# Graph attention on one core: a bound on the gathered index, empty places' logits set by VectorE, and another order of the tiles

## Chip, cores, metric

The kernel runs on one core of one Trainium2 chip. The metric is the device time of one execution in microseconds; the kernel before takes 5479.6 us, the median of three runs (5479.25 to 5485.96).

## What is computed

The input is a graph of 10000 nodes and 170000 edges, sorted by the node that they end in (`dst`); every node has an edge to itself among them. Two graph-attention layers follow each other, with a residual and a normalisation each:

```python
def gat_conv(x, edge_index, W, a_src, a_dst, bias, heads, out_ch, concat):
    xl = (x @ W).reshape(n, heads, out_ch)
    alpha_src = einsum('nhc,hc->nh', xl, a_src)
    alpha_dst = einsum('nhc,hc->nh', xl, a_dst)
    e = leaky_relu(alpha_src[src] + alpha_dst[dst], 0.2)
    e = exp(e - segment_max(e, dst)[dst])
    alpha = e / (segment_sum(e, dst)[dst] + 1e-16)
    return segment_sum(xl[src] * alpha, dst) + bias

h = relu(layer_norm(gat_conv(x, 768 -> 4 heads of 256))) + x @ Wr1 + br1
h = layer_norm(gat_conv(h, 1024 -> 1 head of 768)) + h @ Wr2 + br2
out = layernorm(x + h)
```

All numbers are 32-bit floats. For each node the rows `xl[src]` of its neighbours (17 on average) must be fetched, weighed by the softmax of their logits and added up.

## The kernel before

**Tables and places.** A row of a table holds a node's projected features and its logits: 1024 + 4 + 4 floats in `table1`, 768 + 1 + 1 in `table2`, the source logits first and then the destination logits. One float more in `table1` is the node's rank. Nodes are ranked by falling degree (`prepare`, beside the first projection), and 128 ranks make a tile, 79 in all. A tile t has a fixed number of places n = `SLOTS[t]` for each of its nodes (`slot_counts`, L61): 41 in tile 0, 27 in tile 1, down to 8 in tile 78, 1377 in all. Place 0 is the node itself, the others its neighbours. A node with fewer neighbours than its tile has places points at row `NP` in the places left over. Row `NP` of both tables (`none`, L606 to L611) has features 0 and logits of -1e30, so that its weight becomes 0; its rank field holds `NP`.

**Order.** `TURNS` (L96) is the order in which both layers walk the tiles: 78, 76, ... 0, then 1, 3, ... 77, so the sizes grow from 8 to 41 and fall again to 9. `FIRST[t]` is a tile's first place in that order.

**Ring.** A `Ring` (L434) holds the rows of 28 places in layer 1 and 38 in layer 2 for 128 nodes at once. `fetch` issues one indirect DMA of GpSimd (POOL) for a place: 128 rows, one a partition, named by the column `slots[:, q]` (the gather of L418). A place's gather is issued as soon as the place 28 (or 38) before it has been used up. In layer 2 a tile's own rows lie in a row in `table2`, and SP loads them (L445).

**A tile.** `logits` (L461) adds the source logits of the gathered rows and the tile's own destination logits on VectorE (DVE), for one or two stretches of the ring (`ring.parts`), takes leaky relu and the maximum, and has ScalarE (ACT) take the exponential. In layer 1 ACT also copies the rank field of the gathered rows into `slots` (L478): this is the list of rows that layer 2 gathers, since `table2` is ordered by rank. `normalised` divides the weights by their sum. Then the rows are weighed and added: in layer 1 the first few places of a tile on TensorE through diagonal matrices (L703, L709), of the others one in four by DVE alone (L508) and three by ACT and DVE (L497, L504); in layer 2 512 columns on DVE (L508) and 256 on TensorE (L859, L860). The next tile's logits are taken while this tile is being weighed, if it fits in the ring (L795, L924). Tile 0 doesn't fit and goes through `attend_parts` in three parts.

**Around it.** In layer 1 each tile's sum is normalised (L550 to L566), joined with the residual product (L765), transposed and multiplied by W2 (L169), and stored to `table2` (L730). Layer 2 starts when `table2` is complete. In layer 2 a tile's residual product (L871, L874) uses `h1_d` and a gathered x; DVE adds it on L884, and an indirect DMA of POOL with a bound scatters the result to `out` (L893).

The order of instructions on every engine is that of the program (`manual_schedule`).

Of the kernel before, what the change touches and what calls it, by code (L numbers as in the profile page):

```python
# [78 lines left out]
def gnn_kernel(ctx, tc, x, x_cols, src, dst, src_col, dst_col, W1, a_src1, a_dst1, b1, g1, be1, Wr1, br1,  # L79
               W2, a_src2, a_dst2, b2, g2, be2, Wr2, br2, out, n_edges):  # L80
    nc = tc.nc
    N, D0 = out.shape
    H1, DH1 = a_src1.shape
# [9 lines left out]
    CAPS = slot_counts(N, n_edges)  # L93
    SLOTS = CAPS

    TURNS = list(range(NT - 1, -1, -2))  # L96
    TURNS += sorted(set(range(NT)) - set(TURNS))
    FIRST, TOTAL = [0] * NT, 0
    for t in TURNS:
# [88 lines left out]
    def prepare():  # L188

        with tc.tile_pool(name="prep", bufs=1, side="right") as pool, \  # L190
# [107 lines left out]
                base, s = more, 2 * s  # L298
            nc.vector.tensor_sub(base, base, each)
            rank = pool.tile([P, NT], F32, name="rank")  # L300
            to = pool.tile([P, NT], I32, name="to")
            written = 0

# [33 lines left out]
            with nc.allow_non_contiguous_dma(reason="16 bytes a node"):  # L337
                for to, d in zip([sorted_] + others, order_d):
                    nc.sync.dma_start(to, d.rearrange("(t p) f -> p t f", p=P))
                    yield  # L340
                nc.sync.dma_start(table1[:NP, R1 - 1:].rearrange("(p j) r -> p (j r)", p=P), rank)
                yield
            for other in others:
                nc.vector.tensor_add(sorted_, sorted_, other)
# [89 lines left out]
    class Ring:  # L434

        def __init__(self, pool, table, row, size, own):
            self.table, self.size, self.own, self.issued = table, size, own, 0
            self.rows = pool.tile([P, size, row], F32, name="ring")  # L440

        def fetch(self, upto):
            for q in range(self.issued, min(upto, TOTAL)):
                if q in self.own:
                    nc.sync.dma_start(self.slot(q), self.table[self.own[q] * P:(self.own[q] + 1) * P, :])  # L445
                else:
                    gather(self.slot(q), self.table[:, :], slots[:, q:q + 1])
                self.issued = q + 1

        def slot(self, q):  # L450
# [10 lines left out]
    def logits(small, ring, lo, hi, ad, heads, c, top=None):  # L461


        n = hi - lo
        e = small.tile([P, ring.size, heads], F32, name="e")[:, :n]
        for a, b, rows in ring.parts(lo, hi):
            nc.vector.tensor_tensor(e[:, a - lo:b - lo], rows[:, :, c:c + heads],
                                    ad[:, None, :].to_broadcast([P, b - a, heads]), op=OP.add)
        leaky(e, e)
        new = small.tile([P, heads], F32, name="new")  # L470
        nc.vector.reduce_max(new, e.rearrange("p k h -> p h k"), axis=AX.X)
        if top is not None:
            nc.vector.tensor_max(new, new, top)
        nc.vector.tensor_tensor(e, e, new[:, None, :].to_broadcast([P, n, heads]), op=OP.subtract)  # L474
        nc.scalar.activation(e, e, AF.Exp)  # L475
        if not ring.own:
            for a, b, rows in ring.parts(lo, hi):
                nc.scalar.copy(slots[:, a:b], rows[:, :, R1 - 1])  # L478
        return e, new

    def normalised(small, e, heads, t):
# [109 lines left out]
    with tc.tile_pool(name="w1", bufs=1) as w1p, tc.tile_pool(name="l1", bufs=2) as io, \  # L591
            psum_for_products(), tc.manual_schedule():
        w1 = w1p.tile([P, K0, C1], F32, name="w1")
        xTs = {}

        def load_x(t):
            if t < NT:
                xTs[t] = io.tile([P, K0, P], F32, name="xT", bufs=3)
                nc.sync.dma_start(xTs[t], x_cols[t])

        load_x(0)
        for k in range(K0):
            nc.sync.dma_start(w1[:, k, :], W1[k * P:(k + 1) * P, :])
        load_x(1)
        as_b, ad_b = spread(w1p, a_src1, "as1_b"), spread(w1p, a_dst1, "ad1_b")
        none = w1p.tile([P, R1], F32, name="none")[:1]  # L606
        nc.vector.memset(none[:, :C1], 0.0)
        nc.vector.memset(none[:, C1:], -BIG)
        nc.vector.memset(none[:, R1 - 1:], float(NP))
        nc.scalar.dma_start(table1[NP:NP + 1, :], none)  # L610
        nc.scalar.dma_start(table2[NP:NP + 1, :], none[:, C1 - C2:C1 + 2 * H2])  # L611


        b1_b = w1p.tile([P, R1], F32, name="none")[:, :C1]
        nc.scalar.dma_start(b1_b, bass.AP(tensor=b1.tensor, offset=b1.offset, ap=[[0, P], [1, C1]]))

        def weight_steps():

            with nc.allow_non_contiguous_dma(reason="1024 numbers"):
                nc.scalar.dma_start(br1_c, br1.rearrange("(k p) -> p k", p=P))
            yield
            yield
            brT = spread_br1(w1p, "brT")
            load(w2, W2)
            for i, a in enumerate((a_src2, a_dst2)):
                vec = spread(w1p, a, "a2")
                for k in range(K1):
                    yield  # L630
                    m = io.tile([P, C1], F32, name="scr")[:, :C2]
                    nc.vector.tensor_mul(m, w2[:, k, :C2], vec)
                    nc.scalar.activation(m, m, AF.Copy, accum_out=w2[:, k, C2 + i:C2 + i + 1])
            load(wr1, Wr1)
            yield
            q = product(brT, w2, R2)
            row = io.tile([P, R1], F32, name="row")
            nc.scalar.copy(row[:, :R2], q[:, :R2])
            nc.vector.tensor_add(lift, row[:, C2:C2 + 1], row[:, C2 + 1:R2])
            nc.scalar.dma_start(shift, row[0:1, :C2])  # L640


        steps = itertools.zip_longest(prepare(), weight_steps())
        for t in range(NT):
            p = product(xTs.pop(t), w1, C1)
            row = io.tile([P, R1], F32, name="row")
            nc.scalar.copy(row[:, :C1], p[:, :C1])  # L647
            for i, vec in enumerate((as_b, ad_b)):
# [19 lines left out]
    def ordered_layer1():  # L668
        nonlocal ps_big
        with tc.tile_pool(name="b1", bufs=1) as pool, tc.tile_pool(name="small1", bufs=2) as small, \  # L670
# [20 lines left out]
            def weights_of(t):  # L691

                n, m = SLOTS[t], on_pe(t)
                e, _ = logits(small, ring, FIRST[t], FIRST[t] + n, ring.slot(FIRST[t])[:, C1 + H1:C1 + 2 * H1], H1, C1)
                yield e
                normalised(small, e, H1, t)

# [34 lines left out]
            for t in range(NT + 1):  # L732
# [54 lines left out]
                if live and not whole:  # L787
                    due(n)
                    acc = ps_acc.tile([P, 2 * BANK], F32, name="acc")
                    ad = small.tile([P, H1], F32, name="ad")  # L790
                    nc.vector.tensor_copy(ad, ring.slot(FIRST[t])[:, C1 + H1:C1 + 2 * H1])
# [22 lines left out]
    def ordered_layer2():  # L814
        nonlocal ps_big
        with tc.tile_pool(name="b2", bufs=1) as pool, tc.tile_pool(name="small2", bufs=2) as small, \
# [28 lines left out]
            def weights_of(t):  # L845
# [1 line left out]

                n = SLOTS[t]
                ad = small.tile([P, H2], F32, name="ad")
                nc.vector.tensor_add(ad, ring.slot(FIRST[t])[:, C2 + H2:], lift)  # L850
# [53 lines left out]
            for t in range(NT):  # L904
# [4 lines left out]
                if not whole(t):  # L909
                    for _ in last:  # L910
                        pass
                    ad = small.tile([P, H2], F32, name="ad")
                    nc.vector.tensor_add(ad, ring.slot(FIRST[t])[:, C2 + H2:], lift)
# [34 lines left out]
    def general_path():  # L948
# [82 lines left out]
        def attend_chunks(keep, work, small, lists, table, row, heads, dh, t):  # L1031
# [7 lines left out]
            nc.vector.tensor_copy(top, acc[:, c:c + heads])  # L1039
# [3 lines left out]
            nc.vector.tensor_copy(adm[:, :heads], acc[:, c + heads:c + 2 * heads])  # L1043
# [7 lines left out]
            with tc.For_i(lo, hi, G) as i:  # L1051
# [19 lines left out]
                for g in range(0, G, zg):  # L1071
                    z = work.tile([P, zg, heads, P], F32, name="z")
                    nc.vector.tensor_tensor(
                        z, off[:, g:g + zg, None, :].to_broadcast([P, zg, heads, P]),
                        xg[:, g:g + zg, c:c + heads, None].to_broadcast([P, zg, heads, P]), op=OP.add)
# [22 lines left out]
                nc.vector.tensor_add(e, xg[:, :, c:c + heads], sel[:, :, :heads])  # L1098
# [118 lines left out]
```

## Time and profile before

| | |
|---|---|
| median of three runs | 5479.6 us |
| the profiled execution | 5488.77 us, span 5487.0 us, mean granted clock 0.938 |
| busy share of the span | PE 87%, DVE 79%, POOL 59%, ACT 57% |
| first projection and ranking | 0 to some 905 us |
| layer 1 | some 905 to 3490 us |
| layer 2 | some 3490 to 5487 us |
| DMA packets | 457866, 1581.74 MB, mean 288 GB/s |
| gathers into the ring (L418) | 2675, mean 969 ns of POOL |

The profile is one execution. "Busy" counts the time in which an engine executes; the sequencer's work between two instructions is not in it, and shows as idle time before the next. A wait is put down to the instruction whose signal came last.

### The profile page before, as it was taken

What the parts mean: (1) busy time and instruction counts of PE and PEld (TensorE: products, weight loads), DVE (VectorE), ACT (ScalarE), POOL (GpSimd) and SP (SyncE); (2) the same over time, 40 slices, a digit from 0 to 9 for tenths busy, and PEclk for the clock granted to TensorE, in tenths of its full rate; (3) what the DMA queues carried; (4) which work ended last, traced back from release to release, by engine and by line L of the source; (5) the groups of instructions that cost most, each with busy time, mean ns of one, the idle gap of its engine ahead of it and who ended that gap; (6) DMA issues with size and microseconds to landing.
All of it is one profiled execution on the core that took longest, in us unless ns stands there. A gap on an engine that the chain in (4) does not pass through costs nothing. (4 is left out here: it accounts for less than half of the span.)

```text
span 5487.0 us, 58297 instructions
## 1 busy us (share of the span) xinstructions
PE 4754.0 (87%) x15032; PEld 2827.1 (52%) x15032; DVE 4328.8 (79%) x7766; ACT 3148.0 (57%) x8255; POOL 3247.4 (59%) x3238
## 2 busy tenths in 40 slices
PE   8999997999999875478999999799988746888998
PEld 3444443555555543245555555466655524555665
DVE  5784244899998888788999999498877786778998
ACT  3433344788888877678888888244433312333444
POOL 2445455455566555455665554377777775777774
PEclk9999998999999988789999999899998877899999
DMA  4333625899999988789999997699999987999996
GB/s 152 124 95 82 94 91 202 316 328 339 339 361 347 344 303 301 285 315 345 353 359 347 341 329 263 239 340 360 345 333 321 336 297 258 331 323 349 349 355 240
DMA packets 457866, 1581.74 MB, mean 288 GB/s; under 512 B 111851, under 2 KB 116011, under 8 KB 457526
## 3 DMA queue, kind: packets, MB, share of 16 engines
q0 software_dynamic: 328704, 1339.21, 68.3%
q1 hardware_dynamic: 126768, 235.29, 13.1%
q10 hardware_dynamic: 2054, 3.42, 0.2%
q8 instruction: 126, 2.06, 0.2%
q14 instruction: 214, 1.75, 0.1%
HBM read 1431.80 MB, written 146.23 MB: 288 GB/s over the span
## 5 line engine op out<-in xcount | busy, mean ns | idle before, releaser
L418 POOL DMA_INDIRECT ring<-table,slots x2675 | 2591.7, 969 | 1635.6 <-DVE acc L508 402.4
L508 DVE SCALAR_TENSOR_TENSOR acc<-ring,e,acc 128x256 f32<-128x256 f32 (+1 forms) x2538 | 1572.0, 619 | 127.5 <-PE acc L709 52.0
L497 ACT ACTIVATE ring<-ring,e 128x256 f32<-128x256 f32 x3320 | 1351.0, 505 | 0.0
L504 DVE TENSOR_TENSOR acc<-acc,ring 128x1024 f32<-128x1024 f32 x830 | 1022.5, 1232 | 72.8 <-ACT ring L497 1.2
L874 PE MATMUL big<-wr,w 128*128 128x512 f32 (+1 forms) x2528 | 857.9, 493 | 0.0
L169 PE MATMUL big<-w,xT 128*128 128x512 f32 x1896 | 827.7, 598 | 28.9 <-DMA w<-in_W_dram 11.2
L169 PE MATMUL big<-wr,xT 128*128 128x512 f32 x1896 | 834.1, 596 | 0.7 <-ACT xT L575 0.7
L169 PE MATMUL big<-w,hT 128*128 128x512 f32 (+1 forms) x2528 | 832.1, 486 | 1.2 <-ACT hT L575 1.2
L860 PE MATMUL big<-ring,diagonals 128*128 128x256 f32 x2672 | 660.8, 409 | 185.3 <-ACT diagonals L859 177.0
L860 PEld LDWEIGHTS big<-ring,diagonals 128*128 128x128 f32 x2672 | 543.6, 206 | 299.4 <-ACT diagonals L859 201.2
L169 PEld LDWEIGHTS big<-w,hT 128*128 128x128 f32 x2528 | 478.4, 189 | 375.0 <-issue 341.3
L709 PE MATMUL acc<-ring,diagonals 128*128 128x256 f32 x1816 | 456.6, 409 | 247.9 <-ACT diagonals L703 216.5
L874 PEld LDWEIGHTS big<-wr,w 128*128 128x128 f32 x2528 | 488.1, 193 | 350.3 <-issue 317.7
L169 PEld LDWEIGHTS big<-w,xT 128*128 128x128 f32 x1896 | 362.7, 192 | 491.9 <-issue 472.8
L169 PEld LDWEIGHTS big<-wr,xT 128*128 128x128 f32 x1896 | 356.9, 192 | 421.2 <-issue 420.3
L709 PEld LDWEIGHTS acc<-ring,diagonals 128*128 128x128 f32 x1816 | 370.1, 206 | 326.8 <-ACT diagonals L703 235.7
L859 ACT ACTIVATE diagonals<-ident,e 128x128 f32<-128x128 f32 x1336 | 399.6, 387 | 155.6 <-DVE e L488 117.9
L554 ACT ACTIVATE sd<-mv,eps 128x1 f32<-128x1 f32 x237 | 69.8, 294 | 614.0 <-DVE mv L552 613.6
L650 DVE TENSOR_TENSOR scr<-big,as_b 128x1024 f32<-128x1024 f32 x79 | 96.8, 1225 | 391.9 <-ACT row L647 391.9
L655 POOL TENSOR_TENSOR row<-row,none 128x1024 f32<-128x1024 f32 x79 | 187.2, 2369 | 280.5 <-ACT row L647 279.9
L703 ACT ACTIVATE diagonals<-ident,e 128x128 f32<-128x128 f32 x908 | 278.5, 387 | 96.4 <-DVE e L488 96.4
L475 ACT ACT_TABLE_LOAD x153 | 196.3, 1283 | 233.1 <-DVE e L474 205.9
(172 smaller groups left out, 3895.5 us busy)
## 6 DMA issues: line engine op xcount, KB each, us to landing
ring<-table,slots POOLq DMA_INDIRECT x2675, 6.5
table<-row SPq DMA_DIRECT2D x79, 516.0 KB, 3.6
h_d<-hT SPq DMA_DIRECT2D x79, 512.0 KB, 7.2
w<-h_d SPq DMA_DIRECT2D x79, 512.0 KB, 8.4
table<-row SPq DMA_DIRECT2D x79, 385.0 KB, 6.2
ring<-table SPq DMA_DIRECT2D x79, 385.0 KB, 6.5
xT<-in_x_cols_dram SPq DMA_DIRECT2D x79, 384.0 KB, 4.5
wr<-in_Wr_dram SPq DMA_DIRECT2D x2, 3072.0 KB
```

The costliest lines, as they stand in the source:

```text
L169: nc.tensor.matmul(p[:, c:e], aT[:, j, :], w[:, j, c:e], start=(j == 0), stop=(j == k - 1))
L418: nc.gpsimd.indirect_dma_start(out=to, out_offset=None, in_=table, in_offset=bass.IndirectOffsetOnAxis(ap=index, axis=0), **more)
L475: nc.scalar.activation(e, e, AF.Exp)
L497: nc.scalar.activation(row[:, s], row[:, s], AF.Copy, scale=e[:, h:h + 1])
L504: nc.vector.tensor_add(acc[:, :c], acc[:, :c], row[:, :c])
L508: nc.vector.scalar_tensor_tensor(acc[:, s], row[:, s], e[:, h:h + 1], (acc if first is None else first)[:, s], op0=OP.mult, op1=OP.add)
L655: nc.gpsimd.tensor_add(row[:, :C1], row[:, :C1], b1_b)
L703: nc.scalar.activation(diagonals[:, k * H1 + i, :], ident, AF.Copy, scale=e[:, k, i:i + 1])
L709: nc.tensor.matmul(acc[:, c:d], diagonals[:, k * H1 + i, :], ring.slot(FIRST[t] + k)[:, c:d], start=(k == 0 and c % BANK == 0), stop=(k == ...
L859: nc.scalar.activation(diagonals[:, k % G, :], ident, AF.Copy, scale=e[:, k, :])
L860: nc.tensor.matmul(to, diagonals[:, k % G, :], ring.slot(FIRST[t] + k)[:, ON_PE2:C2], start=False, stop=(k == n - 1), skip_group_check=True)
L874: nc.tensor.matmul(r[:, c:d], hT[:, j, :], wr2[:, j, c:d], start=False, stop=(j == K1 - 1 and (d < C2 or not whole(t))), skip_group_check= ...
```

## The change

Three parts. First, the gathers into the ring get a bound, `NP - 1`: a row whose index is `NP` is not fetched, and the place keeps what it held. The first 28 (or 38) places, which fill the ring, are gathered without the bound. Second, since a place that is not fetched must still have a logit of -1e30, DVE sets the logit columns of the ring to -1e30 once they have been used; for this the destination logits come first in a row now and the source logits second, next to the rank. The rank is stored as a negative number, so that the same -1e30 becomes `NP` by a multiplication with -1 and a minimum with `NP`, which DVE does in place of ACT's copy. Third, `TURNS` becomes 78, 77, ... 48, then 47, 45, ... 1, then 0, 2, ... 46: sizes 8 to 16 in steps of one tile, up to 41, and down to 16.

```diff
-    TURNS = list(range(NT - 1, -1, -2))
+    TURNS = list(range(NT - 1, NT * 3 // 5, -1)) + list(range(NT * 3 // 5, -1, -2))
     TURNS += sorted(set(range(NT)) - set(TURNS))
...
-                nc.sync.dma_start(table1[:NP, R1 - 1:].rearrange("(p j) r -> p (j r)", p=P), rank)
+                nc.vector.tensor_scalar(less_rank, rank, -1.0, None, op0=OP.mult)
+                nc.sync.dma_start(table1[:NP, R1 - 1:].rearrange("(p j) r -> p (j r)", p=P), less_rank)
...
                 if q in self.own:
                     nc.sync.dma_start(self.slot(q), self.table[self.own[q] * P:(self.own[q] + 1) * P, :])
+                elif q < self.size:
+                    gather(self.slot(q), self.table[:, :], slots[:, q:q + 1])
                 else:
-                    gather(self.slot(q), self.table[:, :], slots[:, q:q + 1])
+                    gather(self.slot(q), self.table[:, :], slots[:, q:q + 1], bounds_check=NP - 1,
+                           oob_is_err=False)
...
-            nc.vector.tensor_tensor(e[:, a - lo:b - lo], rows[:, :, c:c + heads],
+            nc.vector.tensor_tensor(e[:, a - lo:b - lo], rows[:, :, c + heads:c + 2 * heads],
                                     ad[:, None, :].to_broadcast([P, b - a, heads]), op=OP.add)
...
         nc.scalar.activation(e, e, AF.Exp)
-        if not ring.own:
-            for a, b, rows in ring.parts(lo, hi):
-                nc.scalar.copy(slots[:, a:b], rows[:, :, R1 - 1])
+        for a, b, rows in ring.parts(lo, hi):
+            if not ring.own:
+                nc.vector.tensor_scalar(slots[:, a:b], rows[:, :, R1 - 1], -1.0, float(NP), op0=OP.mult, op1=OP.min)
+            nc.vector.memset(rows[:, :, c + heads:], -BIG)
...
-        nc.vector.memset(none[:, R1 - 1:], float(NP))
```

The other lines of the diff only swap the two groups of logit columns where they are written and read.

More of the change, by code (lines that the diff above doesn't have):

```diff
@@ L300, in prepare @@
             rank = pool.tile([P, NT], F32, name="rank")
+            less_rank = pool.tile([P, NT], F32, name="less_rank")
             to = pool.tile([P, NT], I32, name="to")
@@ L626, in weight_steps @@
             load(w2, W2)
-            for i, a in enumerate((a_src2, a_dst2)):
+            for i, a in enumerate((a_dst2, a_src2)):
                 vec = spread(w1p, a, "a2")
@@ L647, in gnn_kernel @@
             nc.scalar.copy(row[:, :C1], p[:, :C1])
-            for i, vec in enumerate((as_b, ad_b)):
+            for i, vec in enumerate((ad_b, as_b)):
                 m = io.tile([P, C1], F32, name="scr")
@@ L693, in weights_of @@
                 n, m = SLOTS[t], on_pe(t)
-                e, _ = logits(small, ring, FIRST[t], FIRST[t] + n, ring.slot(FIRST[t])[:, C1 + H1:C1 + 2 * H1], H1, C1)
+                e, _ = logits(small, ring, FIRST[t], FIRST[t] + n, ring.slot(FIRST[t])[:, C1:C1 + H1], H1, C1)
                 yield e
@@ L790, in ordered_layer1 @@
                     ad = small.tile([P, H1], F32, name="ad")
-                    nc.vector.tensor_copy(ad, ring.slot(FIRST[t])[:, C1 + H1:C1 + 2 * H1])
+                    nc.vector.tensor_copy(ad, ring.slot(FIRST[t])[:, C1:C1 + H1])
                     attend_parts(small, ring, acc, acc, ad, None, H1, DH1, t)
@@ L849, in weights_of @@
                 ad = small.tile([P, H2], F32, name="ad")
-                nc.vector.tensor_add(ad, ring.slot(FIRST[t])[:, C2 + H2:], lift)
+                nc.vector.tensor_add(ad, ring.slot(FIRST[t])[:, C2:C2 + H2], lift)
                 e, _ = logits(small, ring, FIRST[t], FIRST[t] + n, ad, H2, C2)
@@ L912, in ordered_layer2 @@
                     ad = small.tile([P, H2], F32, name="ad")
-                    nc.vector.tensor_add(ad, ring.slot(FIRST[t])[:, C2 + H2:], lift)
+                    nc.vector.tensor_add(ad, ring.slot(FIRST[t])[:, C2:C2 + H2], lift)
                     attend_parts(small, ring, h, h, ad, b2_b, H2, DH2, t)
@@ L1038, in attend_chunks @@
             top = keep.tile([P, heads], F32, name="top")
-            nc.vector.tensor_copy(top, acc[:, c:c + heads])
+            nc.vector.tensor_copy(top, acc[:, c + heads:c + 2 * heads])
             total = keep.tile([P, heads], F32, name="total")
@@ L1042, in attend_chunks @@
             adm = keep.tile([P, 2 * heads], F32, name="adm")
-            nc.vector.tensor_copy(adm[:, :heads], acc[:, c + heads:c + 2 * heads])
+            nc.vector.tensor_copy(adm[:, :heads], acc[:, c:c + heads])
             tmp = small.tile([P, heads], F32, name="tmp")
@@ L1074, in attend_chunks @@
                         z, off[:, g:g + zg, None, :].to_broadcast([P, zg, heads, P]),
-                        xg[:, g:g + zg, c:c + heads, None].to_broadcast([P, zg, heads, P]), op=OP.add)
+                        xg[:, g:g + zg, c + heads:c + 2 * heads, None].to_broadcast([P, zg, heads, P]), op=OP.add)
                     pz = ps_tr.tile([P, BANK // P, P], F32, name="tr")
@@ L1097, in attend_chunks @@
                 e = small.tile([P, G, heads], F32, name="ge")
-                nc.vector.tensor_add(e, xg[:, :, c:c + heads], sel[:, :, :heads])
+                nc.vector.tensor_add(e, xg[:, :, c + heads:c + 2 * heads], sel[:, :, :heads])
                 leaky(e, e)
```

## The prediction

> **What bounds the kernel now.** I read the stage windows first, then GpSimd's own timeline, then single lines, and last the tile periods.
>
> The windows split the second layer (3490 to 5487 us) by tile size; after the span the columns are busy us and count of PE, PEld, DVE, ACT and POOL, then granted clock, DMA share and GB/s. The last line is a stretch of the first layer.
>
> ```profile
> 3600.00:3950.00 350.00, 339.31 (x1207) 226.63 (x1206) 310.12 (x666) 151.31 (x361) 264.79 (x276) 0.99 0.97 355
> 3950.00:4440.00 490.00, 399.12 (x1351) 276.79 (x1350) 380.49 (x764) 179.37 (x452) 350.96 (x365) 0.89 0.92 326
> 4600.00:4950.00 350.00, 283.82 (x960) 197.19 (x959) 273.20 (x543) 125.13 (x320) 251.24 (x262) 0.89 0.92 326
> 4950.00:5430.00 480.00, 447.34 (x1541) 293.74 (x1541) 430.96 (x924) 206.97 (x492) 364.61 (x378) 0.96 0.97 355
> ...
> 1300.00:1750.00 450.00, 428.04 (x1460) 258.43 (x1459) 407.64 (x635) 385.90 (x963) 269.33 (x276) 1.00 0.96 350
> ```
>
> POOL looks only three quarters busy. Its timeline says otherwise (start, us, and in brackets the idle time before it):
>
> ```profile
> 5237.93 0.95 POOL L418 DMA_INDIRECT w<-in_x_dram,order  x1 [0.30 <-issue]
> 5239.18 0.96 POOL L418 DMA_INDIRECT ring<-table,slots  x1 [0.30 <-PE big L860]
> 5240.45 1.01 POOL L893 DMA_INDIRECT out_dram<-out,order  x1 [0.30 <-DVE w L884]
> 5241.77 0.97 POOL L418 DMA_INDIRECT ring<-table,slots  x1 [0.30 <-PE big L860]
> 5243.04 0.95 POOL L418 DMA_INDIRECT ring<-table,slots  x1 [0.30 <-DVE acc L508]
> ```
>
> Every indirect DMA takes 0.95 us and 0.30 us of dispatch, whatever is named as releaser: one per 1.25 us. With 0.30 added to each instruction, POOL fills 264.79 + 276 x 0.303 = 348 of 350 us and 479 of 480 in the first and last window, and 94% in the two between. So GpSimd's issue rate bounds most of layer 2. The tile periods (start of L884's addition to the next) agree: 18.9, 20.0, 21.7, 23.2 and 24.3 us on average for tiles of n = 14 to 18 places, against (n - 1 gathers + x + output) x 1.25 = 18.8, 20.0, 21.3, 22.5, 23.8. Below 14, DVE is longer (18.0 busy of 18.05 us at n = 13). From 19 up the period is 1 to 2 us over POOL's sum; there DVE waits for rows.
>
> In layer 1 POOL fills 269.33 + 276 x 0.303 = 353 of 450 us; DVE is 91% busy and up to n = 19 the period is DVE's busy time plus some 1.8 us (26.45 and 28.3 at n = 16). From n = 20 it grows faster (34.9 at 20, 40.8 at 23), as the ring of 28 holds too little of the next tile.
>
> The single lines that price the change (min/median/max ns, then a group's busy, mean and idle time):
>
> ```profile
> L308 POOL DMA_INDIRECT order_d<-facts,to x79: 963/969/1003, 442.7 to 590.2; - x79
> ...
> L893 POOLq MOVE  x79: 29/29/29, 3557.8 to 5468.0; - x79
> ...
> L893 POOL DMA_INDIRECT out_dram<-out,order x79: 982/1022/1688, 3563.5 to 5477.2; - x79
> ...
> L467 DVE TENSOR_TENSOR e<-ring x125: 152/198/267, 923.8 to 3430.0; 128x60 f32<-128x60 f32 x13, 128x52 f32<-128x52 f32 x12, 128x20 f32<-128x20 f32 x11, 128x4 f32<-128x4 f32 x8
> L478 ACT CAST slots<-ring x130: 174/197/234, 925.0 to 3432.5; 128x15 int32<-128x15 f32 x13, 128x13 int32<-128x13 f32 x12, 128x5 int32<-128x5 f32 x11, 128x1 int32<-128x1 f32 x8
> ...
> L491 DVE TENSOR_SCALAR e<-e,loops 128x4 f32<-128x4 f32 x79 | 18.4, 233 | 37.7 <-ACT e L475 37.7
> ```
>
> L893 is the one indirect DMA with a bound today, L308 the scatter without one.
>
> **Part 1, the bound on the index.** No row shows a gather with a bound. From below: zero, because the check may be free in a gather. A gain is excluded, since the first output scatter (112 of its 128 rows lie beyond the last node) takes 1.03 us like the others, so dropped rows do not shorten the instruction. From above: 1022 - 946 = 76 ns (bounded scatter minus layer 2's gather). Between them stands scatter against scatter, 1022 - 969 = 53 ns. I take 53, the like pair. The register move hides in the 0.30 us, which L893 keeps.
>
> In layer 1 this is free: POOL has a fifth to spare, and the cost would show only above 1.6 us an issue. In layer 2 it lands on the bound. The 36 tiles of n = 14 to 18 have 542 gathers: 28.7 us. The 28 tiles of 19 to 27 have 569: 30.2 us, of which I take 70%, 21, since POOL idles 6% there. Tile 0 (n = 41): 1. Tiles below 14 stay on DVE. Sum: **+51 us** (0 to 73).
>
> What it removes: counting from the inputs, 6144 of 176256 places are empty, in only 59 of the 1377 gathers, 29 of them wholly empty. The first ring fill has no bound and holds 998 (layer 1) and 1126 (layer 2) of these, so 5146 x 4132 B + 5018 x 3080 B = 36.7 MB of 1581.74 go. Where POOL or DVE is the bound this is worth nothing. Where data is late, an empty last place lets the logits start up to one issue (1.25 us) sooner. Layer 1, n of 20 and more: nine such tiles, -8. Layer 2, n of 19 and more: eleven, at half, -6. Tile 0 has 1642 empty places; DVE waits 9.3 and 6.6 us for rows around it: -4 and -3. Sum: **-21 us** (-45 to 0).
>
> The Trainium skill speaks against this weighting. "DMA: Bandwidth & Descriptors", section "Anatomy of one DMA", calls descriptor generation small and gives a GpSimd DMA about 2 us plus its bytes at 436 GB/s. By that the bound would cost nothing and 36.7 MB would be 84 us less (an estimate from the page), some 5396 us. The unbroken 1.25 us beat disagrees, so I keep the beat.
>
> **Part 2, more work on DVE.** Layer 1 has 130 stretches of ring; each gets a tensor_scalar into the slots and a memset of five strided columns. The nearest rows are L467's 198 ns (the same strided places) and 157 ns for one column (L850); I take 0.18 each and 0.035 for each hand-over: 130 x 0.43 = 56 us. They stand just where DVE waits for the exponential: L491 idles 37.7 us in all. The cover is 0.48 us a tile; a second stretch (three tiles in five) goes beyond it. 18 us are left; PE, as long as DVE at n = 17 and 18, hides a third: **+12 us** (0 without exposure, 56 without cover). ACT loses 130 x 0.197 = 26 us that nobody waited for. In layer 2 only the memset comes: 0.2 us, hidden while DVE waits for rows (172 us in all), bare in the 14 tiles below n = 14, at 1.3 stretches each: **+4 us** (0 to 23). Behind each memset stand DVE's weighing and then the gathers into those places, but the weighing is later on the same engine, so no new wait arises. The sign change of the rank, one instruction of some 0.2 us, lies beside PE's first stage; swapping the logit columns adds no instruction.
>
> **Part 3, the order.** The same tiles run, and a period depends on n and the next n, which rise and fall as before, so sums hardly change. In layer 1 the last three tiles (11, 11, 9) end with PE behind: 22.4 us pass from the last tile's L765 to the end of its product, of which 5.7 are backlog that a 16-place tile doesn't leave. At the start a 9-place tile then costs PE's 24 us instead of 19.2. Net -1. In layer 2 the last gather leaves at 5425.8, 61 us before the end. With n = 16 last, after it land 6.5 us, 14 of the tile before last, 20.2 for the last tile and 17 of norms and output: 58. I take -5, with POOL's idle start (14 us over the small tiles, more of them now) against it. Sum: **-6 us** (-28 to +10). What SP loads and stores moves with its tile, past nothing else.
>
> **Sum.** 51 - 21 + 12 + 4 - 6 = +40 on the profiled execution (5488.8, span 5487.0). It lay 9.2 above the median of 5479.6, so 5519 (+0.7%).
>
> **Rivals.**
> - *The bound is free and rows count* (faster). The gather has another path than the scatter, and 946 ns stays. For it: nothing in the trace shows a bounded gather; DMA is at 0.92 to 0.97. Against it: L893 against L308. It decides below some 12 ns a gather. Without the 51 us the sum is -11, or -32 if all rows of the big tiles count (3200 x 3080 B at 326 GB/s is 30 us instead of 9): 5448 to 5469, say 5458.
> - *The ends of the layers pay.* From 3400 to 3490 us DMA is a quarter busy. If the order gains its full 28 us and the bound half its price, 40 - 22 - 25 = -7: 5473 to 5487, no change. Against it: layer 1's end waits for PE and DVE, not rows.
> - *DVE has no cover.* All 56 us show: 5563. Against it: 37.7 us of waiting in the very place.
> - *Nothing is dropped*, as descriptors of absent rows still move: 40 + 21 = +61, 5541.
>
> **Chances.** Forecast 0.60, own range 5491 to 5550; free bound 0.20; ends pay 0.12; DVE bare 0.05; nothing dropped 0.03. What a measurement can tell from no change is 0.2%, 11 us. Slower 0.67 (forecast, bare, nothing dropped, less a tail), same 0.13, faster 0.20. The range takes in the free bound and most of the bare DVE: 5447 to 5560.
>
> **What would show it.** Right: L418's median in layer 2 near 1.0 us, beat near 1.30, DVE's waits at L467 longer, layer 2 longer by 30 to 50 us, layer 1 within 15 us; 10164 fewer rows among the DMA packets. L491's idle time falls below 10 us. Wrong: a median that stays at 946 ns; layer 2 shorter; a last gather that leaves much nearer to the end.

## The result, and the profile after

The changed kernel takes 5525.62 us (median of 6 runs, 5515.44 to 5529.43) where the kernel before takes 5484.02 beside it: **1.0079 times as long, interval 1.0068 to 1.009**. The forecast was 5519. The profiled execution took 5525.38 us, with a span of 5523.1 us and a mean granted clock of 0.936.

Three points of the trace divide the span: the first gather of layer 1, the first of layer 2, and the end.

| us | before | after | difference |
|---|---|---|---|
| start to layer 1's first gather | 905.0 | 898.2 | -6.8 |
| layer 1, to layer 2's first gather | 2582.9 | 2572.8 | -10.1 |
| layer 2, to the end of the span | 1999.1 | 2052.1 | +53.0 |

The first row is no effect of the change. In the nine other profiles made on chips of ordinary speed that the same point was read from, it lies at 894.9 to 899.5; only the profile of before is late, which is most of the 9.2 us by which it exceeded its median.

The stage windows of after; the columns are as in the prediction. The first two are stretches of layer 2 without a stop of GpSimd, the third follows tile 0, the last is the stretch of layer 1 shown of before.

```profile
3650.00:4000.00 350.00, 340.58 (x1210) 225.62 (x1209) 311.81 (x709) 152.90 (x361) 269.84 (x264) 1.00 0.94 337
4000.00:4300.00 300.00, 266.95 (x918) 174.38 (x916) 242.57 (x533) 116.77 (x281) 230.83 (x228) 0.95 0.93 333
4950.00:5400.00 450.00, 375.49 (x1262) 258.83 (x1263) 361.92 (x754) 171.12 (x431) 342.68 (x335) 0.89 0.92 324
1300.00:1750.00 450.00, 428.53 (x1419) 251.48 (x1419) 414.14 (x697) 365.37 (x869) 253.38 (x256) 0.99 0.92 323
```

With 0.303 us of dispatch for each instruction, GpSimd fills 269.84 + 264 x 0.303 = 349.8 of 350 us, 299.9 of 300 and 444 of 450: in these stretches it has next to no time to spare, as before. From the first to the last gather of layer 2 it is idle for 69 of 2000 us. In layer 1 it fills 331 of 450. Its timeline shows the beat:

```profile
4149.76 1.00 POOL L421 DMA_INDIRECT ring<-table,slots  x1 [0.30 <-DVE acc L516]
4151.06 1.00 POOL L421 DMA_INDIRECT ring<-table,slots  x1 [0.30 <-issue]
4152.36 1.00 POOL L421 DMA_INDIRECT ring<-table,slots  x1 [0.30 <-DVE acc L516]
```

One gather per 1.306 us (median of layer 2's starts) against 1.250. The dispatch is 0.30 us still, so the register move that comes with the bound (29 ns) is hidden, and the whole difference lies in the instruction. The next two fences are the gathers of a window of each layer (min/median/max ns, then first and last start), layer 1 (960 to 3420 us) and layer 2 (3560 to 5480), first of before, then of after:

```profile
L418 POOL DMA_INDIRECT ring<-table,slots x1337: 932/936/1957, 959.9 to 3397.7; - x191
...
L418 POOL DMA_INDIRECT ring<-table,slots x1251: 940/946/1754, 3561.0 to 5425.8; - x179
```

```profile
L421 POOL DMA_INDIRECT ring<-table,slots x1332: 987/992/1928, 968.8 to 3398.6; - x191
...
L421 POOL DMA_INDIRECT ring<-table,slots x1244: 996/1002/1782, 3559.3 to 5471.4; - x178
```

**56 ns more in both layers.** Sorted by the input's empty places, gathers that drop all 128 rows, some or none have the same median, 992 ns in layer 1 and 1002 ns in layer 2. The last gather of layer 2 leaves at 5471.4 instead of 5425.8.

VectorE's groups in after (busy us, mean ns, then its idle time before them):

```profile
L499 DVE TENSOR_SCALAR e<-e,loops 128x4 f32<-128x4 f32 (+1 forms) x158 | 34.5, 219 | 12.0 <-ACT e L482 9.7
L485 DVE TENSOR_SCALAR slots<-ring 128x7 int32<-128x7 f32 (+17 forms) x128 | 24.7, 193 | 1.0
...
L474 DVE TENSOR_TENSOR e<-ring,ad 128x13 f32<-128x13 f32 (+21 forms) x121 | 20.8, 175 | 269.8 <-DMA ring<-table,slots 214.2 <-issue 43.7 <-DMA out_dram<-out,order 9.7
L486 DVE MEMSET ring<- 128x15 f32 (+31 forms) x244 | 19.5, 87 | 8.0
```

L474 (L467 before) now waits 214.2 us for rows in layer 2, against 172 before. L499's wait for the exponential falls from 37.7 us to at most 9.7: the slots and the memset fill it, as the prediction said (the idle time of the whole group is 12.0 us, where it said below 10).

Last, the packets on the profile's page, first of before, then of after:

```profile
DMA packets 457866, 1581.74 MB, mean 288 GB/s; under 512 B 111851, under 2 KB 116011, under 8 KB 457526
...
q0 software_dynamic: 328704, 1339.21, 68.3%
```

```profile
DMA packets 457885, 1545.22 MB, mean 280 GB/s; under 512 B 119501, under 2 KB 123661, under 8 KB 457526
...
q0 software_dynamic: 328704, 1302.53, 66.4%
```

The 36.7 MB are gone and the number of packets of queue 0 is not. Counted by size, 5146 packets of 4132 B became 5146 of 4 B (9 ns each instead of 161), and of layer 2's packets of 6160 B, two rows each, 2514 are missing and 2504 of 8 B have come. These are the rows that the prediction counted.

### The profile page after: what moved, and what is told of

It is laid out like the page before. It is cut to its first block, busy times and chain, and to the rows that moved or that the text cites. A ratio compares the mean times of both kernels' runs of the same rounds, so it can differ in the third digit from the quotient of the medians.

```text
span 5523.1 us, 60822 instructions
## 1 busy us (share of the span) xinstructions
PE 4756.1 (86%) x15032; PEld 2824.1 (51%) x15032; DVE 4356.9 (79%) x8136; ACT 3134.6 (57%) x8125; POOL 3395.1 (61%) x3238
## 5 line engine op out<-in xcount | busy, mean ns | idle before, releaser
L421 POOL DMA_INDIRECT ring<-table,slots x2675 | 2734.4, 1022 | 1538.4 <-DVE acc L516 368.8
L716 PEld LDWEIGHTS acc<-ring,diagonals 128*128 128x128 f32 x1816 | 365.8, 204 | 313.9 <-ACT diagonals L710 225.2
L657 DVE TENSOR_TENSOR scr<-big,ad_b 128x1024 f32<-128x1024 f32 x79 | 96.7, 1224 | 387.5 <-ACT row L654 387.5
L660 ACT ACTIVATE scr<-scr 128x256 f32<-128x256 f32 x632 | 253.6, 402 | 123.0 <-DVE scr L657 123.0
```

Of the source, the lines that this page charges most:

```text
L421: nc.gpsimd.indirect_dma_start(out=to, out_offset=None, in_=table, in_offset=bass.IndirectOffsetOnAxis(ap=index, axis=0), **more)
L660: nc.scalar.activation(m[:, s], m[:, s], AF.Copy, accum_out=row[:, C1 + i * H1 + h:C1 + i * H1 + h + 1])
L716: nc.tensor.matmul(acc[:, c:d], diagonals[:, k * H1 + i, :], ring.slot(FIRST[t] + k)[:, c:d], start=(k == 0 and c % BANK == 0), stop=(k == ...
```

## The experiments

The theory after the result: the check costs GpSimd some 54 ns a gather, dropped or not; GpSimd's issue bounds layer 2, so it shows there and nowhere else; the dropped rows give some of it back. The rivals: the check is free for the time and order, memset or vector work cost; the DMA engines bound layer 2; dropped rows give nothing.

All times are medians, all ratios to the kernel before on the same chip, each with its interval. Layer times come from the profiled executions, divided as above. They are of one execution each. order_only_2 and bound_in_layer1_2 do the same work in layer 2 and lie at 2007.9 and 2012.8 us there, so a difference of 5 us in a layer means little.

| kernel | time, us | ratio | layer 1 | layer 2 |
|---|---|---|---|---|
| before | 5479 to 5484 | 1 | 2582.9 | 1999.1 |
| after | 5525.62 | 1.0079 | 2572.8 | 2052.1 |
| check_only_2 | 5518.15 | 1.0078 | 2579.3 | 2045.0 |
| no_row_dropped | 5545.63 | 1.0117 | 2586.2 | 2058.0 |
| no_bound_2 | 5499.32 | 1.0048 | 2587.1 | 2013.4 |
| bound_in_layer1_2 | 5485.93 | 1.0013 | 2574.6 | 2012.8 |
| order_only_2 | 5494.37 | 1.0025 | 2583.6 | 2007.9 |
| old_order | 5503.37 | 1.0038 | 2565.9 | 2031.1 |
| x_by_sync | 5445.68 | 0.9941 | 2605.4 | 1943.5 |
| both_reliefs | 5438.70 | 0.9924 | 2593.5 | 1945.6 |

**check_only_2: the check alone, nothing dropped.** The kernel before, with

```diff
-                else:
+                elif q < self.size:
                     gather(self.slot(q), self.table[:, :], slots[:, q:q + 1])
+                else:
+                    gather(self.slot(q), self.table[:, :], slots[:, q:q + 1], bounds_check=NP, oob_is_err=False)
```

> The kernel before with the bound on the index set at NP, so that no row falls outside it, in the order of before. Theory (GpSimd's issue bounds layer 2, and the check itself costs some 54 ns a gather): layer 2 grows by about 1,110 x 54 ns = 60 us less a few that GpSimd had idle, layer 1 by 0 to 8, so 5530 to 5550 us where the kernel before takes 5484 (ratio 1.008 to 1.012). Rival (the check is free for the time, and what cost the change its 41 us is the memset, the vector work or the order of the tiles, none of which is in this kernel): 5480 to 5490, ratio 1.000.

Measured: 5518.15 us, 1.0078 [1.0064, 1.0092]. All 1581.92 MB still move, and the gathers of the two windows take 988 and 998 ns:

```profile
L418 POOL DMA_INDIRECT ring<-table,slots x1333: 984/988/2014, 959.0 to 3389.8; - x191
...
L418 POOL DMA_INDIRECT ring<-table,slots x1248: 992/998/1799, 3559.3 to 5463.0; - x179
```

The time lies 12 us below the theory's range and 28 above the rival's. Layer 1 is 3.6 us shorter, layer 2 45.9 longer. Against the 60 of the expectation, GpSimd's idle time fell. The windows from layer 2's first to its last gather, of before and of check_only_2, say so (GpSimd is the fifth busy time):

```profile
3488.00:5426.00 1938.00, 1620.90 (x5545) 1090.16 (x5546) 1568.41 (x3231) 721.17 (x1770) 1406.44 (x1449) 0.91 0.93 333
```

```profile
3478.00:5463.00 1985.00, 1642.65 (x5546) 1100.49 (x5547) 1569.65 (x3233) 720.59 (x1771) 1476.95 (x1448) 0.90 0.92 325
```

1406.44 + 1449 x 0.303 leaves 93 of 1938 us idle; 1476.95 + 1448 x 0.303 leaves 69 of 1985. So 70.5 us of GpSimd's work came and 24 us of its idle time took a part of it. The rival of a free check falls.

**no_row_dropped: everything of the change but the drop.** The changed kernel, with

```diff
-                    gather(self.slot(q), self.table[:, :], slots[:, q:q + 1], bounds_check=NP - 1,
+                    gather(self.slot(q), self.table[:, :], slots[:, q:q + 1], bounds_check=NP,
```

> The changed kernel with the bound set one row further, at NP, so that every gather is still checked but the row for empty places is fetched as before; order, memset and vector work stay. Theory (the check costs, the dropped rows give 10 to 14 us in layer 1 and 5 to 9 in layer 2): 5538 to 5548 us where the kernel before takes 5480 and the changed one is 1.008 of it (ratio 1.010 to 1.013). Rival (dropping the rows gives nothing, as their packets remain): 5522 to 5528, ratio 1.008.

Measured: 5545.63 us, 1.0117 [1.0102, 1.0133]. Against after, layer 1 is 13.4 us longer and layer 2 5.9: this is what dropping the rows gives in the new order. In the old order it seems to give more in layer 2: old_order, further down, lies 13.9 us below check_only_2 there, with the vector work besides. The rival that it gives nothing falls, though the packets remain.

**no_bound_2: everything of the change but the bound.** The changed kernel, with

```diff
-                elif q < self.size:
+                elif True:
                     gather(self.slot(q), self.table[:, :], slots[:, q:q + 1])
```

> The changed kernel with no bound on any gather: the order of the tiles, the vector work and the -1e30 preset remain, no row is dropped. Theory (the check is the cost): 5470 to 5495 us where the kernel before takes 5484 (ratio 0.997 to 1.002), layer 2 within 10 us of its 1997 us of before. Rival (order, memset and vector work are the cost): 5510 to 5530, ratio 1.005 to 1.009.

Measured: 5499.32 us, 1.0048 [1.0032, 1.0064], between the two expectations: without any bound the kernel is still slower than before, by 21 us between the medians and some 26 by the ratio. In the profiles 4.2 us of it are in layer 1 and 14.3 in layer 2. Against no_row_dropped, which adds only the check, layer 2 is 44.6 us shorter and layer 1 is the same within 1: the check's price once more. So the theory held for the check and missed something beside it: the order, or the vector work.

**bound_in_layer1_2: bound and memset in layer 1 alone.** The changed kernel, with

```diff
-                elif q < self.size:
+                elif q < self.size or self.own:
                     gather(self.slot(q), self.table[:, :], slots[:, q:q + 1])
...
-            nc.vector.memset(rows[:, :, c + heads:], -BIG)
+                nc.vector.memset(rows[:, :, c + heads:], -BIG)
```

(the memset is now under `if not ring.own`).

> The changed kernel with the bound and the memset in layer 1 alone; layer 2's gathers are unbounded. Theory (in layer 1 GpSimd is not the bound, and there the dropped rows give 13 us and the earlier start 7; in layer 2 the check is the cost): 5460 to 5475 us where the kernel before takes 5484 (ratio 0.996 to 0.998), layer 2 as long as before or up to 8 shorter. Rival (layer 1's gain hangs on nothing that is dropped, or layer 2 is longer for its order): 5490 to 5515.

Measured: 5485.93 us, 1.0013 [1.0004, 1.0022]: 11 us above the upper end expected and 4 below the rival's range. Layer 1 is 8.3 us shorter than before's as expected, at gathers of 988 ns, the second line in the next fence showing layer 2's at 946:

```profile
L421 POOL DMA_INDIRECT ring<-table,slots x1332: 984/988/1924, 966.3 to 3399.2; - x191
...
L421 POOL DMA_INDIRECT ring<-table,slots x1244: 940/946/1764, 3561.0 to 5431.6; - x178
```

The "earlier start" of the expectation was the late profile of before, no gain; and layer 2 is 13.7 us longer. No memset runs there, and no_bound_2, which has it, lies 0.6 us apart, so the memset of layer 2 costs nothing that shows, and what is left is the order.

**order_only_2: the order alone.** The kernel before, with

```diff
-    TURNS = list(range(NT - 1, -1, -2))
+    TURNS = list(range(NT - 1, NT * 3 // 5, -1)) + list(range(NT * 3 // 5, -1, -2))
```

> The kernel before with the new order of the tiles and nothing else. Theory (as no_bound_2 and bound_in_layer1_2 show, the new order lets GpSimd stand idle some 17 us more in layer 2 and shortens the tail behind the last gather by 9): layer 2 longer by 10 to 18 us, layer 1 within 5, so 5485 to 5500 us where the kernel before takes 5480 (ratio 1.001 to 1.004). Rival (the 26 us of no_bound_2 come from the vector work in layer 1, the order is a gain as the prediction had it): 5470 to 5480, ratio 0.998 to 1.000.

Measured: 5494.37 us, 1.0025 [1.0015, 1.0036]. The order costs some 12 us. The windows of layer 2: of before from the last gather to the end (the stretch before it stands above, 1938 us), then of order_only_2 both, first to last gather and from there to the end:

```profile
5426.00:5487.00 61.00, 43.70 (x160) 29.44 (x158) 47.20 (x103) 19.63 (x41) 7.79 (x8) 0.90 0.21 74
```

```profile
3479.00:5434.00 1955.00, 1636.57 (x5623) 1102.11 (x5624) 1575.79 (x3255) 728.99 (x1783) 1413.12 (x1453) 0.91 0.92 331
5434.00:5487.00 53.00, 21.88 (x82) 14.98 (x80) 39.72 (x79) 12.12 (x27) 3.91 (x4) 0.74 0.11 40
```

The tail behind the last gather is 8 us shorter, more than the 3 that the prediction counted (61 to 58). But the stretch before it is 17 us longer: GpSimd is idle for 102 us in it instead of 93, and two gathers of x and two outputs more, some 5 us with their dispatch, fall before the last gather instead of behind it. The gain at the end is given back inside. Layer 1 does the same: from its last gather to layer 2's first 73.0 us pass instead of 90.2, and its last gather leaves 17.8 us later, counted from its first; its length is the same.

**old_order: the change without its order.** The changed kernel, with

```diff
-    TURNS = list(range(NT - 1, NT * 3 // 5, -1)) + list(range(NT * 3 // 5, -1, -2))
+    TURNS = list(range(NT - 1, -1, -2))
```

> The changed kernel with the order of the tiles of before; bound, memset and vector work stay. Theory (the order costs 14 us in layer 2 and saves nothing in layer 1): 5505 to 5518 us where the kernel before takes 5480 (ratio 1.005 to 1.007; the changed kernel has 1.008). Rival (the order pays, as the prediction had it, by 6 us): 5528 to 5535, ratio 1.009 to 1.010.

Measured: 5503.37 us, 1.0038 [1.0024, 1.0052], 2 us below the expected range. The changed kernel's ratio is 0.0041 higher, some 22 us. That is more than the 12 of order_only_2, but by the two intervals the 22 are uncertain by some 10 and the 12 by some 6, so it isn't shown that the order costs more here. Both layers have a share (6.9 and 21.0 us), and in layer 2 12 us are more idle time of GpSimd and 14 are longer gathers (mean 1028 instead of 1018 ns, median 1002 instead of 998). If there is more, it stands beside the dropped rows and not beside the check: no_row_dropped and check_only_2, both with the check and without a drop, lie 13.0 us apart in layer 2, much as no_bound_2 and before (14.3). Why the gathers are longer here isn't settled.

**x_by_sync: GpSimd relieved in another place.** The kernel before, with the rows of x stored in order by layer 1 and loaded by SyncE in layer 2:

```diff
+    x_d = dram.tile([NT, P, D0], F32, name="x_d")
...
                     moves = columns(xT, xs[t])
+                    nc.sync.dma_start(x_d[t], xs[t])
...
                 nc.sync.dma_start(hT, h1_d[t])
-                gather(xt, x[:, :], nodes(t))
+                nc.sync.dma_start(xt, x_d[t])
```

> The kernel before, with GpSimd relieved of 43 gathers in layer 2: layer 1 stores each tile's rows of x, in order, to DRAM (one SyncE DMA a tile more in layer 1), and layer 2 loads them by SyncE instead of gathering them again. Theory (GpSimd's issue bounds layer 2 before the change too): 43 x (0.946 + 0.30) us = 54 us come off GpSimd, of which 35 to 50 show, as the other engines are close behind: 5430 to 5450 us where the kernel before takes 5484 (ratio 0.990 to 0.994). Rival (the DMA engines or PE bound layer 2, GpSimd's beat only matches them): 5475 to 5490, since the same bytes move and one store a tile is added. Were the second true, the price of the check could not be a matter of GpSimd's beat.

Measured: 5445.68 us, 0.9941 [0.9927, 0.9955]. The expectation miscounted: there are 79 tiles, not 43, so 79 x 1.25 = 99 us came off GpSimd. Layer 2 is 55.6 us shorter; by the tile periods, which the table further down explains, 28 of them are in the tiles of 14 to 18 places, 21 in tile 0, 7 in those of 19 to 27 and 3 in the smaller ones, less 3 at the ends.

```profile
3500.00:5373.00 1873.00, 1598.81 (x5533) 1087.58 (x5534) 1560.58 (x3213) 719.25 (x1759) 1339.08 (x1371) 0.91 0.94 344
```

78 instructions fewer of GpSimd's, a window 65 us shorter than before's 1938, DMA at 344 GB/s instead of 333, and 118 us of GpSimd idle, so other engines now share the bound. The same bytes for x move in layer 2, so it was not the DMA engines that bounded it. Layer 1, which has the stores, is 22.5 us longer; DMA's share there went from 0.90 to 0.91 and VectorE's wait for rows, without the first of the layer, from 39 to 53 us. What else of the stores costs there was not tried.

**both_reliefs: what the runs point to.** The order of before, bound and memset in layer 1 alone, x by SyncE.

> What the runs point to: the order of before; bound and memset in layer 1 alone, where GpSimd has room; x's rows of layer 2 by SyncE as in x_by_sync. Theory: x_by_sync's 33 us and the 8 to 14 us of layer 1's dropped rows add up, 5430 to 5440 us where the kernel before takes 5480 (ratio 0.991 to 0.993). Rival (layer 1's gain is taken up by the vector work that goes with it, 36 us more of VectorE, or by the stores of x): 5445 to 5452, no better than x_by_sync (ratio 0.994).

Measured: 5438.70 us, 0.9924 [0.991, 0.9938], the fastest kernel of the study. Layer 1 is 11.9 us shorter than in x_by_sync, layer 2 2 us longer. The time is 7 us below x_by_sync's, while the two intervals overlap.

**Four of them on another chip.** check_only, no_bound, order_only and bound_in_layer1 are the kernels of the runs with the same names and a 2, on a chip on which the kernel before itself takes 5841.98 us. Their expectations were written before the order's cost and that chip were known.

> The kernel before, with a bound of NP instead of NP - 1 on the same gathers: every index is inside, so the same rows are fetched and nothing is dropped; no memset, old order. Theory (the check itself costs some 56 ns of GpSimd a gather and layer 2 is bound by GpSimd's issue): gathers at 992 to 1002 ns, layer 2 longer by 50 to 70 us, layer 1 by 0 to 5, in all +50 to +70 us against before. Rival one (the cost comes with rows that are dropped, or with the memsets): gathers at 936 to 946 ns, within 10 us of before. Rival two (the order costs the time in layer 2): also within 10 us.

> The changed kernel with all its gathers unbounded: memsets, DVE's slots and the new order stay, empty places fetch row NP again. Theory: layer 2 gets back 45 to 60 us of the changed kernel's 55 extra, layer 1 loses at most 10 us; total 5470 to 5490 us, within 10 us of before. Rival one (dropping and memsets cost): the memsets stay, so layer 2 stays longer by 20 us or more. Rival two (order): stays near the changed kernel, +30 us or more against before.

> The kernel before with nothing but the new order of the tiles. Theory: -20 to +8 us against before; the end of layer 1 is shorter by some 6 us (PE has no backlog), layer 2 within 10 us. Rival two (order costs in layer 2): +30 to +55 us. A gain of over 20 us would say that the order pays more than the forecast gave it.

> The changed kernel with the bound and the memset in layer 1 only; layer 2 gathers row NP without a bound, the new order stays. Theory: layer 1 as in the changed kernel (12 us shorter than before), layer 2 as with the order alone: -5 to -30 us against before, the fastest of the four. Rival one and rival two: layer 2 stays 30 us or more longer than before.

Measured: check_only 5823.82 us, 0.9965 [0.9953, 0.9977]; no_bound 5846.37, 0.9999 [0.9986, 1.0013]; order_only 5844.41, 1.0003 [0.9992, 1.0015]; bound_in_layer1 5838.74, 0.9992 [0.9979, 1.0005]. The check's 50 to 70 us do not show, and the gain of layer 1's dropped rows is smaller than expected; order_only lies within its range, and no_bound within 10 us of before, but neither tells much where the check itself costs nothing. The reason is in the trace. Layer 2 takes 2314 to 2342 us there. The window of check_only from first to last gather:

```profile
3507.00:5759.00 2252.00, 1735.24 (x5541) 1132.92 (x5542) 1575.07 (x3236) 733.78 (x1773) 1479.21 (x1449) 0.85 0.83 287
```

1479.21 + 1449 x 0.303 leaves GpSimd 334 us idle. PE is late there: its timeline (order_only) shows single multiplications of 0.38 us with 1.5 to 2.5 us before each, in which it waited for nothing that the profile shows:

```profile
5320.02 0.38 PE L860 MATMUL big<-ring,diagonals 128*128 128x256 f32 x1 [1.56 <-issue]
5322.85 0.38 PE L860 MATMUL big<-ring,diagonals 128*128 128x256 f32 x1 [2.45 <-issue]
```

From 3550 to 5750 us such waits of PE in check_only come to over 350 us; in check_only_2, the same kernel, the list of PE's waits in layer 2 has none. The granted clock between the first and the last gather is 0.85 there and 0.90 here. What holds PE up on that chip isn't settled, nor why check_only is 0.35% faster there. But the gathers cost the same (988 and 998 ns with the check, 936 and 946 without), and where GpSimd has 334 us to spare, 52 ns on each gather of layer 2 cost nothing that shows. So the price of the check is paid only where GpSimd's beat is the bound.

## Why the prediction was right

The direction, the size and the main mechanism, the check on GpSimd's beat, were right; one term had the wrong sign, others were off by as much in the other direction, and the bound of the small tiles was misread. A tile's period runs from the addition on L884 (L891 in after) of the tile before it to its own. The periods of layer 2, summed by size, show each term (us):

| | to the first tile's L884 (L891 in after) | n up to 13 | 14 to 18 | 19 to 27 | tile 0 | rest |
|---|---|---|---|---|---|---|
| before | 58.8 | 218.1 | 782.4 | 826.9 | 98.7 | 14.1 |
| check_only_2 | 58.7 | 221.9 | 810.5 | 838.7 | 101.2 | 14.0 |
| order_only_2 | 59.3 | 225.3 | 780.9 | 830.4 | 98.1 | 14.0 |
| no_bound_2 | 59.4 | 225.2 | 778.9 | 837.0 | 98.9 | 14.0 |
| no_row_dropped | 58.7 | 226.8 | 810.1 | 846.8 | 101.6 | 14.0 |
| after | 58.6 | 226.6 | 809.8 | 840.7 | 102.2 | 14.3 |

- **Bound, +51: measured +46 and +45.** The pair chosen (bounded against unbounded scatter, 53 ns) was the right one: 52 ns in check_only_2, 56 in after. The tiles of 14 to 18 took 28.1 us where 28.7 stood. The tiles of 19 to 27 were mis-sized: 11.8 instead of 21. Their 569 gathers grew by 30 us, of which 40% and not 70% show, probably since VectorE's waits for rows and GpSimd's idle time leave more room there. x_by_sync says the same: these tiles lost one gather of 1.25 us each, 35 us, and became 7 shorter. Tile 0 has 2.5 instead of 1, the small tiles 3.8 instead of 0.
- **In layer 1 the check costs nothing**: -3.6 us in check_only_2, and no_row_dropped and no_bound_2 within 1 us, as said.
- **Dropped rows, -21: measured -19** (13.4 and 5.9). Layer 1's 12 and the -6 of the tiles above 18 (846.8 to 840.7) hold; tile 0's -3 does not (101.6 to 102.2). The reason of an earlier arrival agrees: in after, gathers that drop all 128 rows land after 4.25 us in layer 1 (median of those whose landing the trace has; 7.13 before) and 4.87 in layer 2 (6.65 before).
- **Vector work in layer 1, +12: measured some +3.5 in the profiles** (no_bound_2 against order_only_2, within the scatter). The whole times of these two, on different chips, are 8 to 13 us apart with an uncertainty of some 10, so how much of the 12 and of the next term shows isn't settled. The work itself was 24.7 us for L485 and, by bound_in_layer1_2's group, 13.2 for the memsets of layer 1, so 38 instead of 56, and the wait for the exponential covered most (28 us of it are gone).
- **Memset in layer 2, +4: measured 0.6**, no more than the scatter. The prediction let it show in the tiles below 14 places, where it took VectorE for the bound ("18.0 busy of 18.05 us at n = 13"). The engine without idle time there is PE. The next lines are a tile of 13 places and one of 9, of before (the 9 is the last tile) and then of after (the 9 is the second); the busy times are again PE, PEld, DVE, ACT and POOL:

```profile
3613.43:3631.47 18.04, 18.04 (x66) 11.95 (x65) 16.87 (x38) 8.41 (x19) 13.22 (x15) 1.00 0.97 341
5462.16:5472.86 10.70, 7.54 (x34) 5.76 (x32) 10.28 (x21) 1.62 (x3) 0.98 (x1) 1.00 0.11 40
```

```profile
3682.65:3700.70 18.05, 18.05 (x66) 11.96 (x65) 16.79 (x39) 8.20 (x19) 13.84 (x14) 1.00 0.95 336
3529.58:3544.38 14.80, 14.80 (x54) 9.87 (x53) 13.93 (x35) 6.69 (x16) 10.23 (x10) 1.00 0.84 293
```

With the memset or without it, the tile of 13 takes 18.0 us (in no_bound_2 and order_only_2 too); VectorE is busy for 16.8 to 16.9 of them and has room. Nor did these tiles gain much in x_by_sync, 3 us of 218, so GpSimd was hardly their bound either. (Two readings beside this one are off, and nothing rests on them: at n = 14 the mean period is 19.2 us and 18.9 the median, and in layer 1 VectorE is busy for 26.0 us at n = 16, not 26.45.)

- **Order, -6: measured +12 by the medians of order_only_2, and +22 against old_order.** This step failed: "a period depends on n and the next n, which rise and fall as before, so sums hardly change". Sums did change: the tiles of up to 13 places take 7 us more, since all now stand at the start of the layer, where before half of them ran at the end. The tile of 9 places took 10.7 us there, as the last tile, with PE busy for 7.5 of them (34 multiplications, as the last tile has no next tile's product beside it); in after it takes 14.8 with PE busy throughout (54 multiplications, the lines above). And the tiles of 19 and more take 3.5 more, within the scatter of one profile (bound_in_layer1_2 and no_bound_2 have 7 and 10 more). The gain at the end was there, and larger than counted. The prediction had set the idle start "against it", and that was the larger part. For layer 1, where -1 stood, order_only_2 says +1.

By these figures the errors of order (some 18 us up) and of vector work, memset and bound (8, 3 and 5 us down) leave +42 where +40 was forecast. The nearness of the sum is in part luck. Of the signs named, the median, the beat and layer 1 came as said; layer 2 grew by 53 us, just over the 30 to 50, and the 10164 rows went from the bytes but not from the packet count.

Of the rivals, "the bound is free" fails by the gathers' own duration, "the ends pay" because the ends' gain is given back, "DVE has no cover" because well under half of its 56 us shows. "Nothing is dropped" fails for the time, though its reason, descriptors of absent rows that still move, is true in another form: a packet remains, 9 ns long.

The Trainium skill's "DMA: Bandwidth & Descriptors", section "Anatomy of one DMA", calls descriptor generation small; the estimate from its bandwidth was 84 us less for the dropped rows. The runs bear out neither what the prediction drew from the first, a bound that costs nothing, nor the second: the check lengthens GpSimd's instruction by 52 to 56 ns and layer 2 by 46 us with no byte changed, and the 36.7 MB are worth 19 us.

## What to carry to other kernels

Where an engine issues indirect DMAs back to back, its beat (instruction and dispatch) is the bound even if the profile calls it three quarters busy, and each nanosecond on every issue counts: here 52 ns times some 1250 made 46 us, while 36.7 MB less to move made 19. So skip rows only where the issuing engine has room (layer 1), and where it has none take whole instructions off its queue: 79 gathers handed to SyncE shortened layer 2 by 56 us and lengthened layer 1 by 22.5, where the rows had to be stored first, 33 us less in all. An order that makes the end cheaper has to be summed over the whole layer, since the small tiles it moves away from the end cost more where they go. And before a period is put down to an engine, its idle time in that very period has to be read: in the small tiles PE had none, and VectorE over 1 us.

## What the runs showed that was not expected

- A row that the bound drops is still a packet: 4 B in 9 ns instead of 4132 B in 161 ns. Some 5146 x 152 ns / 16 = 49 us per DMA engine went in layer 1 (an estimate from these numbers), and 13 us came of it.
- The check's price is in the instruction alone and doesn't depend on what is dropped: 988 ns (check_only_2, nothing dropped) and 992 (after) against 936 in layer 1.
- The medians differ by 3 to 4 ns without a change in the gathers: 998 ns in layer 2 in check_only_2 and old_order, 1002 in after and no_row_dropped. It doesn't take another order of the tiles: one kernel, bound_in_layer1 and bound_in_layer1_2, has 992 and 949 ns (layers 1 and 2) on one chip and 988 and 946 on the other. No run explains it.
- The same kernel takes 5842 us on one chip and 5480 on others. Of the four kernels profiled on both, layer 1 is 25 to 35 us longer there and layer 2 269 to 328.
